# Moving the last attention unit's output into the FFN, the first block's transposes into attention's tail, and one norm's root to GpSimd

## The chip, the cores and the metric

The kernel runs on one core of a Trainium2 chip. A core has five engines that take their own instructions in order: TensorE (PE, matmuls into the eight PSUM banks), VectorE (DVE), ScalarE (ACT, activations by table), GpSimd (POOL) and SyncE (SP, whose queue issues most of the DMAs). They wait for each other by semaphores. The metric is the device time of one execution in microseconds (us). Three runs of the kernel before took 3608.94, 3609.37 and 3612.33 us; the median is 3609.37.

## The reference

One layer of a transformer over 4096 tokens of width 256, in f32: attention with 16 heads, a post-norm, a gated FFN with ternary weights and two hidden layers of 1024, and a second post-norm.

```python
proj = quant4(x) @ ternary_weight(Wqkv_w).T + Wqkv_b
q = proj.reshape(B, N, h, dk).transpose(0, 2, 1, 3)
k = proj.reshape(B, h, N, dk)
v = proj.reshape(B, h, N, dk)
q, k = (rotary(q, N), rotary(k, N))
ql, kl = (q @ U, k @ U)
att = jnp.einsum('bhnr,bhmr->bhnm', ql, kl) / math.sqrt(dk)
y = jax.nn.softmax(att, axis=-1) @ v
y = y.transpose(0, 2, 1, 3).reshape(B, N, d)
x = _layernorm(x + quant4(y) @ ternary_weight(Wo_w).T)
...
h = jax.nn.silu(_tlin(x, w1_w, w1_s)) * _tlin(x, w2_w, w2_s)
h = jax.nn.gelu(_tlin(h, h1_w, h1_s), approximate=False)
h = jax.nn.gelu(_tlin(h, h2_w, h2_s), approximate=False)
x = _layernorm(x + _tlin(h, w3_w, w3_s))
```

`quant4` rounds each row to integers from -8 to 7 by its largest magnitude. `_layernorm` subtracts the mean and divides by the square root of the variance plus 1e-5. `_tlin` is a product with a weight matrix, scaled per output.

## The kernel before

**Attention** works on 64 units: a unit is a pair of heads (8 pairs) and a block of 512 queries (8 blocks). A unit has 32 steps, one for each 128 keys. At a step, `largest` finds the largest score of some rows (PE, then DVE's reduction at L605), and 40 steps later (`LAG`) `weights` computes the scores anew with that largest subtracted (PE, L643) and ACT takes the exponential into a tile `pr` (L651) of the pool `ppool`, which has eight buffers. `values` multiplies two steps' exponentials by the values (PE, L665) at the odd steps, 5 steps behind, into the bank `av`.

When a unit's values are complete, its output is put in order: `finish` (ACT copies `av` into `ya`, L680), eight calls of `turn` (DVE transposes `ya` into `yt` in 32x32 squares, L686), `gather` (SP writes `yt` to DRAM as `y_raw` in four DMAs, L694, and reads it back as `y4`, L699), `add_strips` (POOL adds two halves, L707) and `divide` (DVE takes the reciprocal of the softmax's sum, L716; POOL multiplies, L718; SP stores to `y_dram`, L724).

The order of all this is written out by hand. `at(step, f)` puts a function into a list of that step; the loop at L890 runs over the steps, calls the listed functions and then issues `largest` and `weights`. On each engine the instructions stand in the order in which this loop issues them. `last` is the step number 2048, where the last unit's `largest` ends; the loop goes on to step `last` + 47, with the `weights` of the last 40 steps up to `last` + 39. This stretch is the tail. For the units before the last the pieces of the output's ordering are spread over later steps; for the last unit (`gap` = 0) they come at once, at steps `last` + 45 and `last` + 47.

The tail also prepares the first block of the FFN, 512 tokens. `front_steps(0)` gives seven pieces, put at steps `last` + 2 to `last` + 22: the attention result is quantised on DVE, transposed on PE, multiplied by the output weights, added to x, and normalised: `measure` (mean and variance on DVE, L212), `root` (ACT's square root, L216) and `scale` (DVE, L220 and L222).

**The FFN** follows in a branch: a flag that attention's checks of the weights have set chooses the form (L1055). With these inputs it is the form `split`, in which each f32 operand is held as two f32r parts, high and low. It runs over eight blocks of 512 tokens, again in an order written out by hand. A block has gates (eight pairs of products with w1 and w2, by `o` = 0 to 7; Silu on ACT, product on DVE), two hidden layers h1 and h2 (eight products each with Gelu) and the last layer w3 (two products). A product's matmuls are at L945 and take one of eight PSUM banks. `parts` writes the high part (ACT or DVE, L927) and the low part (DVE, L929). `transpose_x` turns a block of x for the gates (eight PE transposes, L961); for block 0 it stands first in the FFN (L1004). The `front_steps` of the next block are spread over the present block: its load of `y_dram` (`yb`, SP) behind gate `o` = 4, its quantisation behind h1's `o` = 1, its transposes behind `o` = 4.

The weights are loaded by `load_weights` on POOL's queue: w1, w2 and h1 during attention; h2 (4 MB) and w3 (1 MB) at L911 to L913 when the FFN begins, into memory that attention frees. The first half of h2 waits for the last reading of the keys, the second for that of the values.

Of the kernel before, what the change touches and what calls it, by code (L numbers as in the profile page):

```python
# [18 lines left out]
P = 128  # L19
N = 4096  # L20
D = 256
# [16 lines left out]
def attn_ffn_kernel(  # L38
# [31 lines left out]
    make_identity(nc, ident)  # L70
    identb = const.tile([P, P], BF16, name="identb")
    make_identity(nc, identb)

    identr = const.tile([P, P], F32R, name="identr")
    nc.gpsimd.tensor_copy(identr, ident)
    ones = const.tile([P, P], F32, name="ones")
    nc.gpsimd.memset(ones, 1.0)
    eps = const.tile([P, 1], F32, name="eps")
    nc.gpsimd.memset(eps, LN_EPS)

    most = const.tile([P, BT, 2], F32, name="most")
    nc.gpsimd.memset(most, 1e-6)
# [118 lines left out]
    def load_x(b):  # L201
        nc.sync.dma_start(out=xs[b], in_=x_t[:, ts(b, BT), :])

    def layernorm_steps(t):

        mv = stat.tile([P, BT, 2], F32, name="mv")
        sd = stat.tile([P, BT], F32, name="sd")

        def measure():
            for i in range(BT):  # L210
                st = stat.tile([P, 6], F32, name="st")
                nc.vector.bn_stats(st, t[:, i, :])  # L212
                nc.vector.bn_aggr(mv[:, i, :], st)

        def root():
            nc.scalar.activation(sd, mv[:, :, 1], AF.Sqrt, bias=eps)  # L216

        def scale():
            rs = stat.tile([P, BT], F32, name="rs")
            nc.vector.reciprocal(rs, sd)  # L220
            for i in range(BT):
                nc.vector.tensor_scalar(  # L222
                    t[:, i, :],
                    t[:, i, :],
                    mv[:, i, 0:1],
                    rs[:, i : i + 1],
                    ALU.subtract,
                    ALU.mult,
                )

        return measure, root, scale

    def front_steps(b, bank):

        xb = xs[b]
        yb = quantp.tile([P, BT, D], F32, name="yb")
        nc.sync.dma_start(out=yb, in_=y_dram[b].rearrange("(t p) d -> p t d", p=P))

        def evacuate(i, ps, ma7):
            o = quantp.tile([P, D], F32, name="o", bufs=2)  # L240
            nc.vector.scalar_tensor_tensor(o, ps, ma7, alpha_o, ALU.mult, ALU.mult)
            nc.gpsimd.tensor_tensor(xb[:, i, :], xb[:, i, :], o, ALU.add)

        held, biggest, measure_y, quantized, transposed = quantize_steps(yb, bank, nc.vector)

        def integers():
            biggest(None)
            for f in measure_y:
                f()
            quantized()  # L250

        measure, root, scale = layernorm_steps(xb)
        return [
            integers,
            transposed,
            lambda: project(held, sgn_o, bank, 0, evacuate),
            lambda: project(held, sgn_o, bank, 2, evacuate),
            measure,
            root,
            scale,  # L260
        ]


    with ExitStack() as actx:
# [23 lines left out]
        m_dram = [dram.tile([32, P], F32, name=f"m_dram{i}") for i in range(2)]  # L288

        qpool = actx.enter_context(tc.tile_pool(name="qpool", bufs=2))  # L290
        ppool = actx.enter_context(tc.tile_pool(name="ppool", bufs=8))
        ps_sc = actx.enter_context(tc.tile_pool(name="ps_sc", bufs=2, space=PSUM))
        ps_av = actx.enter_context(tc.tile_pool(name="ps_av", bufs=1, space=PSUM))
        ps_1 = actx.enter_context(tc.tile_pool(name="ps_1", bufs=3, space=PSUM))
# [290 lines left out]
        def at(step, f):  # L585
            todo.setdefault(step, []).append(f)
# [89 lines left out]
        def finish(u):  # L676


            yas[u] = qpool.tile([P, QB], F32, name="ya", bufs=1)
            nc.scalar.copy(yas[u], avs.pop(u))  # L680
            yts[u] = qpool.tile([P, QB], F32, name="yt", bufs=1)

        def turn(u, i):

# [3 lines left out]
        def gather(u):  # L688

            del yas[u]  # L690
            raw = y_raw[u % 2]
            yt = yts.pop(u).rearrange("p (b e) -> p b e", e=32)
            for strip in range(4):
                nc.sync.dma_start(  # L694
                    out=raw.rearrange("(b q) s e -> s q b e", q=32)[strip],
                    in_=yt[32 * strip : 32 * strip + 32],
                )
            y4s[u] = qpool.tile([P, BT, 2, 2, 32], F32, name="y4", bufs=1)
            nc.sync.dma_start(  # L699
                out=y4s[u].rearrange("p t j k e -> p t (j k e)"),  # L700
                in_=raw.rearrange("(t p) s e -> p t (s e)", p=P),
            )

        def add_strips(u):
            y4 = y4s.pop(u)
            ys[u] = qpool.tile([P, BT, 2, DK + 1], F32, name="y", bufs=1)
            nc.gpsimd.tensor_tensor(  # L707
                ys[u], y4[:, :, :, 0, : DK + 1], y4[:, :, :, 1, : DK + 1], ALU.add
            )

        def divide(u):

            pair, qb = divmod(u, NQB)
            y = ys.pop(u)
            den = stat.tile([P, BT, 2], F32, name="den")
            nc.vector.reciprocal(den, y[:, :, :, DK])  # L716
            yu = stat.tile([P, BT, 2, DK], F32, name="yu")
            nc.gpsimd.tensor_tensor(  # L718
                yu,
                y[:, :, :, :DK],  # L720
                den.unsqueeze(3).broadcast_to([P, BT, 2, DK]),
                ALU.mult,
            )
            nc.sync.dma_start(  # L724
                out=y_dram[qb].rearrange("(t p) d -> p t d", p=P)[
                    :, :, pair * 32 : (pair + 1) * 32
                ],
                in_=yu.rearrange("p t j e -> p t (j e)"),
            )
# [33 lines left out]
        with tc.manual_schedule():  # L763
# [70 lines left out]
            for u in range(NU):  # L834
# [18 lines left out]
                at(NKT * (u + 1) + 3, lambda u=u: largest_rows(u))  # L853
                end = base + NKT + AVLAG - 1
                at(end, lambda u=u: finish(u))
                gap = 2 if u < NU - 1 else 0
                for i in range(8):
                    at(end + 2 + gap * i, lambda u=u, i=i: turn(u, i))
                at(end + 2 + 8 * gap, lambda u=u: gather(u))
                at(end + 4 + 11 * gap, lambda u=u: add_strips(u))  # L860
                at(end + 4 + 12 * gap, lambda u=u: divide(u))
            last = NKT * NU
            at(last - 240, lambda: load_weights(w1_sb, w1T, 0))
            w2_sb, h1_sb, h2_sb = [None, None], [None, None], [None, None]
# [19 lines left out]
            def start_front():  # L884
                steps = front_steps(0, lambda shape, dt: ps_1.tile(shape, dt, name="ps1"))
                for i, f in zip((0, 6, 10, 12, 16, 18, 20), steps):
                    at(last + 2 + i, f)

            at(last - 60, start_front)
            for s in range(NKT * NU + LAG + AVLAG + 4):  # L890
                while todo.get(s):
# [10 lines left out]
    with ExitStack() as fctx:  # L902
# [4 lines left out]

        h2_sb[0] = kpool.tile([P, NC // 2, DH], F32R, name="h2a", tag="kT")
        h2_sb[1] = wpool2.tile([P, NC // 2, DH], F32R, name="h2b")
        w3_sb = wpool2.tile([P, NC, D], F32R, name="w3_sb")  # L910
        for i in range(2):  # L911
            load_weights(h2_sb[i], h2T, i * NC // 2)
        load_weights(w3_sb, w3T, 0)  # L913

        def bank(shape, dt):
            return psum.tile(shape, dt, name="ps_mm")
# [1 line left out]
        def ffn(split):  # L918
# [2 lines left out]
            np_ = 2 if split else 1  # L921
            dt = F32R if split else F32
            nb = NT // BT

            def parts(dst, k, g, eng):

                eng(dst[:, k, 0, :], g)  # L927
                if split:
                    nc.vector.tensor_tensor(  # L929
                        dst[:, k, 1, :], g, dst[:, k, 0, :].bitcast(F32), ALU.subtract  # L930
                    )

            def product(w, o, src):
                ps = bank([P, 512], F32)
# [16 lines left out]
                        )  # L951
                return ps

            xTs, fTs = {}, {}

            def transpose_x(b):
                xTs[b] = tmp.tile([P, 2, np_, BT * P], dt, name="xT", bufs=1)
                for k in range(2):
                    ps = bank([P, 512], F32)
                    for i in range(BT):  # L960
                        nc.tensor.transpose(ps[:, ts(i, P)], xs[b][:, i, ts(k, P)], ident)  # L961
                    parts(xTs[b], k, ps, nc.scalar.copy)

            def gates(b, o, ha):
                pa = product(((w1_sb,), w1T), o, xTs[b])
# [9 lines left out]
            def hidden(w, sc, o, ha, hb):  # L975
                ps = product(w, o, ha)
                g = tmp.tile([P, BT * P], F32, name="gate", bufs=3) if split else hb[:, o, 0, :]
                nc.scalar.activation(g, ps, AF.Gelu, scale=scales[sc][:, o : o + 1])  # L978
                if split:
                    parts(hb, o, g, nc.vector.tensor_copy)  # L980

            def last_layer(b, o, ha):
                ps = product(((w3_sb,), w3T), o, ha)
# [17 lines left out]
            def hlayer():  # L1001
                return hpool.tile([P, NC, np_, BT * P], dt, name="h")

            transpose_x(0)  # L1004
            for b in range(nb):
                fronts = ends = None
                ha = hlayer()
# [1 line left out]
                for o in range(NC + 1):  # L1009

                    held, g = g, gates(b, o, ha) if o < NC else None
                    if o and split:
                        parts(ha, o - 1, held, nc.scalar.copy)
                    if b and o < 2:
                        add_up(b - 1, o)
                    if o == 4 and b + 1 < nb:
                        fronts = front_steps(b + 1, bank)
                if b:
                    ends = layernorm_steps(xs[b - 1])
                hb = hlayer()  # L1020
                for o in range(NC):
                    hidden((h1_sb, h1T), "hs1", o, ha, hb)
                    if o == 0 and ends:
                        ends[0]()
                    if fronts:
                        step = {1: 0, 4: 1, 5: 2, 6: 3, 7: 4}.get(o)
                        if step is not None:
                            fronts[step]()
                ha, hb = hb, hlayer()
                for o in range(NC):  # L1030
# [12 lines left out]
                    if o == 1 and b + 2 < nb:  # L1043
                        load_x(b + 2)
                    if o == 3 and b + 1 < nb:
                        transpose_x(b + 1)
                for o in range(2):
                    last_layer(b, o, hb)
            for o in range(2):
# [67 lines left out]
```

## Time and profile before

| what | value |
|---|---|
| median of three runs | 3609.37 us |
| the profiled execution: time, span | 3610.68 us, 3608.9 us |
| mean granted TensorE clock | 0.989 |
| busy: PE, DVE, ACT, POOL | 3553.8, 3044.0, 2340.4, 429.1 us |
| last exponential of the tail starts | 2911.95 us |
| last matmul of attention ends | 2914.1 us |
| first matmul of h1, block 0 | 2948.50 us |
| DMA rate, 2920 to 2930 us | 291 GB/s |

Times within the profile are counted from the start of the span. In a row of instructions the first two numbers are the start and the duration; then come the engine, the line of the kernel, the operation, what it writes and reads with the shapes, and how many were merged. What stands in brackets is how long the engine was idle before, and what ended that. In the chain of work that ended last, each piece is followed back to what released it. PEclk is the share of TensorE's full clock that was granted in that stretch.

### The profile page before, as it was taken

How to read it: one execution, taken by the hardware profiler on the slowest of the kernel's cores; microseconds unless marked ns; L12 is line 12 of the kernel's file. 1: busy time of each engine (PE TensorE's matmuls, PEld its weight loads, DVE VectorE, ACT ScalarE, POOL GpSimd, SP SyncE). 2: the span in 40 equal slices, each digit the busy share in tenths (PEclk: the TensorE clock that was granted, in tenths of full speed). 3: DMA queues.
4: the chain of work that ended last, by engine and by line, in shares of the span. 5: the costliest groups of instructions: out<-in, count | busy, mean ns of one | idle time of the engine just before them, and what ended most of it. 6: DMA issues, size and time to landing. Idle time of an engine off the chain costs nothing.

```text
span 3608.9 us, 61076 instructions
## 1 busy us (share of the span) xinstructions
PE 3553.8 (98%) x23831; PEld 2000.3 (55%) x23831; DVE 3044.0 (84%) x5611; ACT 2340.4 (65%) x2715; POOL 429.1 (12%) x515
## 2 busy tenths in 40 slices
PE   8999999999999999999999999999999979999998
PEld 4444555555545555555555555455555458888887
DVE  8888999999999999999999999999999735555544
ACT  2777777777777777777777777777777743333333
POOL 5666300000000000000000000000000000000000
PEclk7999999999999999999999999999999989999999
DMA  3343212111211121111111111200221030000000
GB/s 88 93 111 101 59 26 50 26 27 26 53 29 27 27 50 28 28 42 34 26 26 44 34 29 28 50 21 21 55 59 38 15 89 1 24 30 18 18 7 13
DMA packets 267634, 141.74 MB, mean 39 GB/s; under 512 B 184520, under 2 KB 243656, under 8 KB 266440
## 3 DMA queue, kind: packets, MB, share of 16 engines
q1 hardware_dynamic: 263512, 126.22, 14.0%
q0 software_dynamic: 3824, 11.54, 1.0%
q8 instruction: 189, 3.10, 0.4%
q14 instruction: 109, 0.89, 0.1%
HBM read 91.44 MB, written 42.07 MB: 37 GB/s over the span
## 4 chain that ended last, share of the span: by engine, by line
PE 93%; DVE 2%; DMA 2%; POOL 2%; ACT 1%; issue 0%; SPq 0%; POOLq 0%; DVEq 0%; ACTq 0%
PE av L665 27%; PE sc L643 25%; PE ps L597 21%; PE ps_mm L945 18%; DVE mx L605 1%; PE ps L494 0%; DMA qT<-q_dram 0%; DMA y_raw<-yt 0%; DMA ma_dram<-ma_turned 0%; DMA kT<-k_dram 0%; PE ps L424 0%; DMA scale<-ma_dram 0%; POOL qk L457 0%; PE sc L523 0%; PE ps L171 0%
## 5 line engine op out<-in xcount | busy, mean ns | idle before, releaser
L605 DVE TENSOR_REDUCE mx<-ps 128x1 f32<-128x512 f32 x4096 | 2549.8, 682 | 149.0 <-PE ps L597 94.3
L651 ACT ACTIVATE pr<-sc 128x1024 f32<-128x1024 f32 x2048 | 1991.4, 1021 | 739.4 <-PE sc L643 737.5
L597 PEld LDWEIGHTS ps<-kT,qT 64*128 64x128 f32 x4096 | 568.7, 185 | 983.4 <-DVE mx L605 851.2
L665 PE MATMUL av<-pr,v_all 128*32 128x512 f32 x8192 | 1091.9, 605 | 0.0
L597 PE MATMUL ps<-kT,qT 64*128 64x512 f32 x4096 | 1068.2, 475 | 6.2 <-DMA qT<-q_dram 1.7
L643 PE MATMUL sc<-m_rows,minus 64*128 64x512 f32 x4096 | 823.7, 395 | 3.9 <-ACT pr L651 3.5
L643 PE MATMUL sc<-qT,kT 64*128 64x512 f32 x4096 | 818.2, 392 | 0.0
L643 PEld LDWEIGHTS sc<-m_rows,minus 64*128 64x128 f32 x4096 | 393.6, 185 | 91.7 <-ACT pr L651 40.9
L643 PEld LDWEIGHTS sc<-qT,kT 64*128 64x128 f32 x4096 | 394.0, 185 | 86.5
L665 PEld LDWEIGHTS av<-pr,v_all 128*32 128x32 f32 x8192 | 161.4, 108 | 257.9 <-issue 256.1
L978 ACT ACTIVATE gate<-ps_mm,sc_hs 128x512 f32<-128x512 f32 x128 | 88.0, 688 | 288.9 <-PE ps_mm L945 248.5
L927 DVE CAST h<-gate 128x512 fp32r<-128x512 f32 x128 | 54.3, 425 | 223.7 <-ACT gate L978 223.6
L618 POOL TENSOR_TENSOR m_parts<-m,m_parts 128x8 fp32r<-128x8 f32 x64 | 12.9, 202 | 1800.3 <-ACT m_parts L617 1765.1
L929 DVE TENSOR_TENSOR h<-gate,h 128x512 fp32r<-128x512 f32 x192 | 132.3, 689 | 5.1
L686 DVE STREAM_TRANSPOSE yt<-ya 128x64 f32<-128x64 f32 x512 | 118.1, 232 | 17.9 <-ACT ya L680 17.9
L945 PE MATMUL ps_mm<-h,h1a 128*128 128x512 f32 x512 | 128.9, 394 | 0.0
L945 PE MATMUL ps_mm<-h,h2a 128*128 128x512 f32 x512 | 127.2, 390 | 0.0
L945 PE MATMUL ps_mm<-h,h2b 128*128 128x512 f32 x512 | 126.5, 389 | 0.0
L945 PE MATMUL ps_mm<-h,h1b 128*128 128x512 f32 x512 | 126.5, 389 | 0.0
L970 DVE SCALAR_TENSOR_TENSOR gate<-ps_mm,sc_s,gate 128x512 f32<-128x512 f32 x64 | 48.0, 750 | 83.2 <-ACT gate L968 58.0
L945 PEld LDWEIGHTS ps_mm<-h,h1b 128*128 128x128 f32 x512 | 96.1, 188 | 20.1
L945 PEld LDWEIGHTS ps_mm<-h,h2b 128*128 128x128 f32 x512 | 96.1, 188 | 20.0
(160 smaller groups left out, 1640.9 us busy)
## 6 DMA issues: line engine op xcount, KB each, us to landing
y_raw<-yt SPq DMA_DIRECT2D x256, 64.0 KB
y<-y_raw SPq DMA_DIRECT2D x64, 256.0 KB
qT<-q_dram SPq DMA_DIRECT2D x252, 64.0 KB
kT<-k_dram SPq DMA_DIRECT2D x28, 512.0 KB
xs<-in_x SPq DMA_DIRECT2D x16, 512.0 KB
q_dram<-qk SPq DMA_DIRECT2D x32, 256.0 KB
k_dram<-qk SPq DMA_DIRECT2D x56, 128.0 KB
cs_q<-in_csq SPq DMA_DIRECT2D x8, 512.0 KB
```

The costliest lines, as they stand in the source:

```text
L597: nc.tensor.matmul(ps[j], lhsT=qTs[u][rows, ts(qt, P)], rhs=kTs[u // NQB][rows, ts(ck, 512)], start=True, stop=True,)
L605: nc.vector.tensor_reduce(mxs[u][:, qt, j, ck : ck + 1], ps[j], AX.X, ALU.max)
L618: nc.gpsimd.tensor_tensor(parts[:, :, 1, :], m, parts[:, :, 0, :].bitcast(F32), ALU.subtract)
L643: nc.tensor.matmul(ps[:, j, :], lhsT=minus[rows, :] if first else kTs[u // NQB][rows, ts(kt, P)], rhs=m_rows[u % 2][rows, :] if first else ...
L651: nc.scalar.activation(pr, ps, AF.Exp)
L665: nc.tensor.matmul(avs[u][strip : strip + 32, :], lhsT=v_all[:, 2 * (2 * pair + j) + a, c * (DK + 1) : c * (DK + 1) + 32], rhs=probs[s + k ...
L686: nc.vector.transpose(yts[u][:, ts(i, 64)], yas[u][:, ts(i, 64)])
L927: eng(dst[:, k, 0, :], g)
L929: nc.vector.tensor_tensor(dst[:, k, 1, :], g, dst[:, k, 0, :].bitcast(F32), ALU.subtract)
L945: nc.tensor.matmul(ps, lhsT=sb[:, ks, ts(o, P)] if split else wo[:, k, :], rhs=src[:, k, i, :], start=(k == 0 and i == 0), stop=(k == n - ...
L970: nc.vector.scalar_tensor_tensor(g, pb, scales["s2"][:, o : o + 1], gate, ALU.mult, ALU.mult)
L978: nc.scalar.activation(g, ps, AF.Gelu, scale=scales[sc][:, o : o + 1])
```

## The change

1. The last unit's output is no longer ordered in attention's tail, apart from ACT's copy `ya`. Its turns, its DMAs, its addition and its division go into the first block of the FFN: the turns and `gather` behind gate `o` = 1, `add_strips` behind h1's `o` = 2, `divide` behind `o` = 3. Its tiles come to lie in memory that lives on: `ya` and `y4` in the third buffer of x, `yt` in a tile of the quantisation.
2. Block 0's x is transposed in the tail, at steps `last` + 28 and `last` + 30, into the memory of w3, which moves into a pool that lives from the start; DVE writes the high part there instead of ACT. w3 is loaded behind block 0's gates. To make room, `ppool` has six buffers instead of eight and `yu` two instead of four.
3. The root of block 0's first norm is taken by POOL: variance plus 1e-5, raised to the power -0.5, then two rounds of four operations that refine it. ACT's square root and DVE's reciprocal go for this one norm.
4. An identity in f32r that nothing used goes; a constant of -0.5 comes.

```diff
-    identr = const.tile([P, P], F32R, name="identr")
-    nc.gpsimd.tensor_copy(identr, ident)
...
+    minus_half = const.tile([P, BT], F32, name="minus_half")
+    nc.gpsimd.memset(minus_half, -0.5)
...
-    def layernorm_steps(t):
+    def layernorm_steps(t, between=False):
...
         def root():
-            nc.scalar.activation(sd, mv[:, :, 1], AF.Sqrt, bias=eps)
+            if not between:
+                nc.scalar.activation(sd, mv[:, :, 1], AF.Sqrt, bias=eps)
+                return
+            nc.gpsimd.tensor_scalar(sd, mv[:, :, 1], LN_EPS, None, ALU.add)
+            r = stat.tile([P, BT], F32, name="rs")
+            nc.gpsimd.tensor_tensor(r, sd, minus_half, ALU.pow)
+            for _ in range(2):
+                e = stat.tile([P, BT], F32, name="rse")
+                nc.gpsimd.tensor_tensor(e, r, r, ALU.mult)
+                nc.gpsimd.tensor_tensor(e, e, sd, ALU.mult)
+                nc.gpsimd.tensor_scalar(e, e, -0.5, 1.5, ALU.mult, ALU.add)
+                nc.gpsimd.tensor_tensor(r, r, e, ALU.mult)
+            inv.append(r)
...
-        measure, root, scale = layernorm_steps(xb)
+        measure, root, scale = layernorm_steps(xb, b == 0)
...
+    def transpose_x(b, k, xT, split, bank, eng):
+        ps = bank([P, 512], F32)
+        for i in range(BT):
+            nc.tensor.transpose(ps[:, ts(i, P)], xs[b][:, i, ts(k, P)], ident)
+        parts(xT, k, ps, split, eng)
+
+    left = []
+
+    w3_sb = wpool.tile([P, NC, D], F32R, name="w3_sb")
+    xTs = {0: w3_sb.rearrange("p (k i a) d -> p k i (a d)", k=2, i=2)}
+    last_unit = x_bufs[2].rearrange("p i d -> p (i d)")
...
-        ppool = actx.enter_context(tc.tile_pool(name="ppool", bufs=8))
+        ppool = actx.enter_context(tc.tile_pool(name="ppool", bufs=6))
...
+        def turn_last():
+            yas[NU - 1] = last_unit[:, :QB]
+            yts[NU - 1] = quantp.tile([P, BT * D], F32, name="yt", tag="qtmp")[:, :QB]
+            for i in range(8):
+                turn(NU - 1, i)
+            gather(NU - 1)
...
-                gap = 2 if u < NU - 1 else 0
+                if u == NU - 1:
+                    left += [turn_last, lambda u=u: add_strips(u), lambda u=u: divide(u)]
+                    continue
...
+                def first_xT(k):
+                    transpose_x(0, k, xTs[0], True, bank1, nc.vector.tensor_copy)
+
+                for k in range(2):
+                    at(last + 28 + 2 * k, lambda k=k: first_xT(k))
...
-        w3_sb = wpool2.tile([P, NC, D], F32R, name="w3_sb")
         for i in range(2):
             load_weights(h2_sb[i], h2T, i * NC // 2)
-        load_weights(w3_sb, w3T, 0)
...
-            transpose_x(0)
+            if not split:
+                next_xT(0)
...
                     if o and split:
-                        parts(ha, o - 1, held, nc.scalar.copy)
+                        parts(ha, o - 1, held, split, nc.scalar.copy)
+                    if not b and o == 1:
+                        left[0]()
...
+                if not b and split:
+                    load_weights(w3_sb, w3T, 0)
...
+                    if not b and o in (2, 3):
+                        left[o - 1]()
```

More of the change, by code (lines that the diff above doesn't have):

```diff
@@ L202, in load_x @@
         nc.sync.dma_start(out=xs[b], in_=x_t[:, ts(b, BT), :])
-    def layernorm_steps(t):
+    def layernorm_steps(t, between=False):
         mv = stat.tile([P, BT, 2], F32, name="mv")
         sd = stat.tile([P, BT], F32, name="sd")
+        inv = []
         def measure():
@@ L215, in root @@
         def root():
-            nc.scalar.activation(sd, mv[:, :, 1], AF.Sqrt, bias=eps)
-        def scale():
-            rs = stat.tile([P, BT], F32, name="rs")
-            nc.vector.reciprocal(rs, sd)
+            if not between:
[11 more added lines that the diff above has]
+            inv.append(r)
+        def scale():
+            if between:
+                rs = inv.pop()
+            else:
+                rs = stat.tile([P, BT], F32, name="rs")
+                nc.vector.reciprocal(rs, sd)
             for i in range(BT):
@@ L261, in front_steps, with parts @@
         ]
+    def parts(dst, k, g, split, eng):
+        eng(dst[:, k, 0, :], g)
+        if split:
+            nc.vector.tensor_tensor(dst[:, k, 1, :], g, dst[:, k, 0, :].bitcast(F32), ALU.subtract)
+    def transpose_x(b, k, xT, split, bank, eng):
[7 more added lines that the diff above has]
+    last_unit = x_bufs[2].rearrange("p i d -> p (i d)")
     with ExitStack() as actx:
@@ L676, in finish @@
         def finish(u):
-            yas[u] = qpool.tile([P, QB], F32, name="ya", bufs=1)
+            if u < NU - 1:
+                yas[u] = qpool.tile([P, QB], F32, name="ya", bufs=1)
+            else:
+                yas[u] = last_unit[:, :QB]
             nc.scalar.copy(yas[u], avs.pop(u))
-            yts[u] = qpool.tile([P, QB], F32, name="yt", bufs=1)
+            if u < NU - 1:
+                yts[u] = qpool.tile([P, QB], F32, name="yt", bufs=1)
+        def turn_last():
[4 more added lines that the diff above has]
+            gather(NU - 1)
         def turn(u, i):
@@ L697, in gather @@
                 )
-            y4s[u] = qpool.tile([P, BT, 2, 2, 32], F32, name="y4", bufs=1)
+            if u < NU - 1:
+                y4s[u] = qpool.tile([P, BT, 2, 2, 32], F32, name="y4", bufs=1)
+            else:
+                y4s[u] = last_unit[:, QB:].rearrange(
+                    "p (t j k e) -> p t j k e", t=BT, j=2, k=2
+                )
             nc.sync.dma_start(
@@ L705, in add_strips @@
             y4 = y4s.pop(u)
-            ys[u] = qpool.tile([P, BT, 2, DK + 1], F32, name="y", bufs=1)
+            if u < NU - 1:
+                ys[u] = qpool.tile([P, BT, 2, DK + 1], F32, name="y", bufs=1)
+            else:
+                ys[u] = y4[:, :, :, 0, : DK + 1]
             nc.gpsimd.tensor_tensor(
@@ L716, in divide @@
             nc.vector.reciprocal(den, y[:, :, :, DK])
-            yu = stat.tile([P, BT, 2, DK], F32, name="yu")
+            yu = stat.tile([P, BT, 2, DK], F32, name="yu", bufs=2)
             nc.gpsimd.tensor_tensor(
@@ L855, in attn_ffn_kernel @@
                 at(end, lambda u=u: finish(u))
-                gap = 2 if u < NU - 1 else 0
+                if u == NU - 1:
+                    left += [turn_last, lambda u=u: add_strips(u), lambda u=u: divide(u)]
+                    continue
                 for i in range(8):
[L858 to L861, printed above, removed]
+                    at(end + 2 + 2 * i, lambda u=u, i=i: turn(u, i))
+                at(end + 18, lambda u=u: gather(u))
+                at(end + 26, lambda u=u: add_strips(u))
+                at(end + 28, lambda u=u: divide(u))
             last = NKT * NU
@@ L923, in ffn @@
             nb = NT // BT
[L925 to L931, printed above, removed]
             def product(w, o, src):
@@ L952, in product, with next_xT @@
                 return ps
-            xTs, fTs = {}, {}
-            def transpose_x(b):
+            fTs = {}
+            def next_xT(b):
                 xTs[b] = tmp.tile([P, 2, np_, BT * P], dt, name="xT", bufs=1)
                 for k in range(2):
[L959 to L962, printed above, removed]
+                    transpose_x(b, k, xTs[b], split, bank, nc.scalar.copy)
             def gates(b, o, ha):
@@ L979, in hidden @@
                 if split:
-                    parts(hb, o, g, nc.vector.tensor_copy)
+                    parts(hb, o, g, split, nc.vector.tensor_copy)
             def last_layer(b, o, ha):
@@ L1045, in ffn @@
                     if o == 3 and b + 1 < nb:
-                        transpose_x(b + 1)
+                        next_xT(b + 1)
                 for o in range(2):
```

## The prediction

> **What bounds the kernel now.** I first read the page's strip of forty slices (90.2 us each). TensorE (PE) is at 9 tenths in nearly all of them. What the change can win lies where it is not: in the eighth slice from the right, 2887 to 2977 us, where attention gives over to the FFN and the granted clock dips too. There I read the chain that ended last, in order of time, then the instructions of ScalarE (ACT) in order, then PE's.
>
> The strip, one character a slice:
>
> ```profile
> PE   8999999999999999999999999999999979999998
> PEclk7999999999999999999999999999999989999999
> ```
>
> The chain across the join (start, duration, what):
>
> ```profile
> 2911.85 2.27 PE av L665 x16
> ...
> 2914.15 0.59 ACT ya L680
> ...
> 2914.76 1.14 DVE yt L686 x8
> ...
> 2917.46 10.10 DMA y_raw<-yt
> ...
> 2927.68 2.91 DMA y<-y_raw
> ...
> 2930.73 0.48 POOL y L707
> ...
> 2931.24 0.21 DVE den L716
> ...
> 2931.98 0.70 DVE xT L929
> 2932.68 0.04 issue
> 2932.72 34.07 PE ps_mm L945 x143
> ```
>
> PE's attention work ends at 2914.1 and the FFN's products run from 2932.7. Between them stands the last unit's output: turned, sent to DRAM, fetched, added, divided. No FFN product needs that output; block 7 alone does. It holds PE because VectorE (DVE) takes its instructions in order, and the division's reciprocal (den, L716) stands ahead of the low half of the first block's transposed x (xT, L929). PE's own rows, the last of them being the first matmul of the second layer (h1):
>
> ```profile
> 2916.19 0.50 PE L945 MATMUL ps_mm<-xT,w_sb 128*128 128x512 f32 x1 [0.29 <-ACT xT L927]
> 2932.72 1.65 PE L945 MATMUL ps_mm<-xT,w_sb 128*128 128x512 f32 x3 [16.03 <-DVE xT L929]
> ...
> 2948.50 1.98 PE L945 MATMUL ps_mm<-h,h1a 128*128 128x512 f32 x8
> ```
>
> The stop costs twice: the granted clock in the windows of 1 us is 0.50 from 2932 to 2935, and three matmuls take 1.65 us where four take 1.07 later.
>
> ACT's rows in attention's tail, where the norm's root is:
>
> ```profile
> 2885.20 1.02 ACT L651 ACTIVATE pr<-sc 128x1024 f32<-128x1024 f32 x1 [0.43 <-PE sc L643]
> 2886.24 1.28 ACT L216 ACT_TABLE_LOAD   x1
> 2887.54 0.30 ACT L216 ACTIVATE sd<-mv,eps 128x4 f32<-128x4 f32 x1
> 2887.85 1.28 ACT L651 ACT_TABLE_LOAD   x1
> 2889.15 2.94 ACT L651 ACTIVATE pr<-sc 128x1024 f32<-128x1024 f32 x3
> 2893.78 1.94 ACT L651 ACTIVATE pr<-sc 128x1024 f32<-128x1024 f32 x2 [1.69 <-PE sc L643]
> ```
>
> A root of 512 values stops the exponentials for two table loads; PE runs dry behind it, and the granted clock is 0.50 from 2892 to 2894.
>
> **The change part by part.**
>
> *The join, gain 19.2.* Before, from the end of the last av (2914.1) to the first matmul of the second layer (2948.5): 34.4 us. After it, nothing of the last unit stands ahead of the gates, and both halves of xT lie ready. PE's gap from its last av to its next instruction is 0.74 us today, and I keep it. A pair of gate products then costs 1.81 us (w1's products start at 2939.43 and 2941.24); eight pairs are 14.5. New: 0.74 + 14.5 = 15.2; gain 34.4 - 15.2 = 19.2. The FFN's eight transposes in front of the gates are in the 34.4 and so go as well. ACT's Silu table load (1.28 us), which hid in the stop, now stands behind the copy of ya, 0.59 us of copy, some 0.4 of branch (as DVE's two entries L1055 and L1056 took) and the load: 2.3 after av, 1.6 after PE starts. With eight PSUM banks PE needs no bank back before four pairs, 7.2 us: no cost. If that cover were gone it would cost 1.3.
>
> *Where the moved work goes.* Eight turns (1.13 us of DVE) come after the first parts of the gates (o = 1). DVE is asked for 0.75 + 0.68 = 1.43 us per pair of 1.81 there, so it recovers 0.38 a pair, three pairs, within the four of the banks: 0, at worst 1.1. SP (SyncE's queue): the four writes of y_raw start near 2918 (the end of av moves to 2914.1 - 4.3 + 0.9 = 2910.7 by the terms below; then 0.74, two pairs, and 0.75 + 0.69 + 1.13 of DVE); today they took 11.6 us (2915.92 to 2927.56) beside the loads of h2 and w3, and 3.6 for the unit before (2889.89 to 2893.45). So the fetch of y4, and behind it on SP the load of yb of block 1, go out between 2922 and 2930. Who waits: DVE's quantisation of yb, today from 2957.74 to 2962.8 (5.1 us), and PE's transposes of it at 2966.63. Both move 22.6 earlier, the transposes to 2944.0, so yb must be there by 2939, 9 us after the latest issue; a DVE that waits until then is late only for the second layer's outputs, which the third layer needs. POOL's large loads landed in 3.1 to 10.5 us, so 0, at worst 1.5 of PE time. The additions and the reciprocal (hidden layer, o = 2 and 3) come some 10 us after the latest y4 issue, which took 2.9: 0.
>
> *w3.* Its four issues (0.74 us each) move on POOL from the join to behind the gates, where they wait for PE's last reading of xT; behind them on POOL stand the strip addition and the adds of block 1, needed only from 2942 on. Its first use is after both hidden layers, some 58 us later (16 products of 3.63); landing 10.5 at most: 0.
>
> *The root, gain 4.3.* Undisturbed, pairs of exponentials start 2.12 and 2.37 us apart in turn (2898.48, 2900.85, 2902.97, 2905.34). From the exponential at 2885.20 to the last, at 2911.95, there are 21, ten such distances: 22.45, so the last would start at 2907.65. Gain 4.30, of which some 3.0 is ACT's stop and the rest PE's slow clock and refill.
>
> The Trainium skill (ScalarE: Activation LUTs, What ACT_TABLE_LOAD costs) gives a switch of tables 1.28 us of load and 1.38 of drain, 2.66 in all. By it two switches would be an estimated 5.3 for this term and the sum 1.0 larger; the rows show the same load, but the next instruction 0.02 us behind it, so I do not take its figure.
>
> POOL's replacement is ten instructions: an add, the power, and two rounds of four. The nearest rows are POOL's 128x8 operations at 0.20 us (m_parts, L618), so 2.0 us; the other end is POOL's slowest small one, 1.22 us (L345), so 12.2. The mean is ready at 2881.7; the scaling (1.38) must end before PE comes to the first moved transpose. That stands ahead of the scores of an exponential nine after the one at 2885.20, which by those distances starts at 2895.1, its scores some 2 us before: 2893. So POOL has about 10 us. By the near row 8 are left; by the far one PE waits 2.2. I take 0. No row shows a power.
>
> The Trainium skill (GPSIMD Engine Reference, Instruction dispatch) says that the first call to a freshly loaded kernel pays about 6 us. If power were one, the estimate would be 8 us on POOL, still inside the slack, and the sum unchanged; no row of this trace can show it.
>
> *The moved transposes, loss 0.9.* Eight f32 transposes now stand among the tail's scores. Eight take 0.87 to 1.06 us on PE. The nearest row is the output projection in the same tail, twice 0.54: around it pairs go from 2875.14 to 2880.71, 5.6 where two distances are 4.5, so such work is paid in full there. Ends 0 and 1.1; I take 0.9. Their copies (0.43 and 0.69 on DVE, twice) meet a DVE that is idle 6.8 us in this tail: 0.
>
> *Six instead of eight probability buffers.* The exponential of step s overwrites that of s-6, whose av products stand on PE before the scores that this exponential waits for anyway. So 0 by the order in the code; a fault here would be multiplied by 2048. Set-up takes seven of these tiles, and the seventh falls on tw[0], whose readers stand ahead on the same DVE: 0. The identity that goes and the constant that comes are 0.28 and about 0.1 us of POOL, off the chain: 0.
>
> *Sum.* 19.2 + 4.3 - 0.9 = 22.6. The profiled execution took 3610.68 (span 3608.9), 1.3 above the median of 3609.37. 3610.68 - 22.6 = 3588.1, and against the median **3587**.
>
> **The rivals.**
>
> 1. *The gates are slowed by the burst of loads.* Now the gates run while the 4 MB of h2 come in, at a DMA share that was 1.04 in the idle stretch 2920 to 2930. For it: y_raw took 8 us longer there than one unit earlier; code and descriptors of the engines could be late alike, as could yb. Against it: from 2933 to 2938 PE ran gates at a DMA share of 1.0 to 1.1 without gaps. At 8 us late: 22.6 - 8 = 14.6, time 3595.
>
> 2. *POOL's power is late.* With 1.22 us an instruction PE waits 2.2 us; if it is longer still, the root's whole gain goes: 22.6 - 4.3 = 18.3, time 3591.
>
> 3. *The join's wait is replaced.* The first gates might wait for something else: memory of attention's pools under the h and gate tiles, or a bank. For it: PE's first FFN instruction began just as the copy of ya ended (2914.73). Against it: the same row shows this is 0.74 us. If as much as 16 us stayed, the time would be 3603.
>
> 4. *Slower: the probability buffers bind.* If ACT has to wait for a buffer at each step, 2048 exponentials multiply it: 11 ns each (22.6 / 2048) cancels all, 20 ns gives 3587 + 41 = 3628. Against it: the order above, and ACT's waits over the whole span name the scores alone (us in total, times, longest), with no row for av:
>
> ```profile
> ACT pr L651 <- PE sc L643: 737.5, 1020, 2.4
> ```
>
> **How the numbers follow.** My forecast has 0.80, rival 1 0.09, rival 2 0.04, rival 3 0.03, rival 4 0.04. Faster by over 0.2% (7.2 us, about what a measurement of this kernel can tell from no change) are the forecast, rivals 1 and 2, and rival 3 where less stays (0.01): 0.94; within 0.2% the rest of rival 3: 0.02; slower rival 4: 0.04. The range: below, transposes hidden (0.9) and the spread of the runs (0.4 under the median), with a slightly shorter join: 3584. Above, to rival 1 with a little: 3596. That leaves out rival 3, 4 and a tail of the first.
>
> **What would show it.** Right: in the chain, ps_mm L945 follows av within about 1 us and no y_raw stands on it; no table load between the exponentials of the tail; the second layer's first matmul near 2926; the granted clock at 1.00 through the join. Wrong: a PE wait on DVE xs or POOL ahead of the transposes (rival 2), gaps among the gate products (1 or 3), ACT waits on PE av from the first units on, with a pair of steps over today's (4).

## The result, and the profile after

The changed kernel takes 3588.37 us (median; 3586.83 to 3590.5), the kernel before 3609.77 beside it (five runs, the three of the section on its time among them): a ratio of 0.9938, 95% interval 0.9928 to 0.9949, 21.4 us less (18.4 to 26.0 by the interval). The prediction said 3587, with a range of 3584 to 3596.

The profiled execution took 3586.87 us (span 3585.0). In the page's strip of forty slices the dip in the eighth slice from the right is gone from both rows:

```profile
PE   7999999999999999999999999999999999999998
PEclk7999999999999999999999999999999999999999
```

The chain across the join (start, duration, what), which before held the writes and the fetch of the last unit:

```profile
2907.03 2.27 PE av L700 x16
2909.30 0.02 issue
2909.32 0.59 ACT xs L718
2909.92 0.04 issue
2909.96 32.95 PE ps_mm L997 x144
```

PE now goes from attention's last product (av) to the gates with one copy between (ya, which now lies in a buffer of x and bears that name). PE's own rows, start and duration first, as they answer to those shown of before:

```profile
2909.96 1.20 PE L997 MATMUL ps_mm<-w_sb 128*128 128x512 f32 x4 [0.69 <-ACT xs L718]
...
2924.62 1.98 PE L997 MATMUL ps_mm<-h,h1a 128*128 128x512 f32 x8
```

The wait of 16.03 us for DVE is gone; a wait of 0.69 us for the copy ya is left, where it was 0.74. The granted clock is 1.00 in every window that I read from 2890 to 2940 us. The first matmul of h1 comes 15.3 us after the end of av, where it was 34.4. ACT's rows at the place where the table loads stood:

```profile
2883.38 1.94 ACT L686 ACTIVATE pr<-sc 128x1024 f32<-128x1024 f32 x2 [0.43 <-PE sc L678]
2885.50 1.94 ACT L686 ACTIVATE pr<-sc 128x1024 f32<-128x1024 f32 x2 [0.18 <-PE sc L678]
2887.86 1.94 ACT L686 ACTIVATE pr<-sc 128x1024 f32<-128x1024 f32 x2 [0.42 <-PE sc L678]
2889.99 1.94 ACT L686 ACTIVATE pr<-sc 128x1024 f32<-128x1024 f32 x2 [0.19 <-PE sc L678]
2892.35 1.03 ACT L686 ACTIVATE pr<-sc 128x1024 f32<-128x1024 f32 x1 [0.42 <-PE sc L678]
2893.60 1.02 ACT L686 ACTIVATE pr<-sc 128x1024 f32<-128x1024 f32 x1 [0.23 <-PE sc L678]
2895.25 1.03 ACT L686 ACTIVATE pr<-sc 128x1024 f32<-128x1024 f32 x1 [0.63 <-PE sc L678]
2896.51 1.02 ACT L686 ACTIVATE pr<-sc 128x1024 f32<-128x1024 f32 x1 [0.23 <-PE sc L678]
2898.16 1.94 ACT L686 ACTIVATE pr<-sc 128x1024 f32<-128x1024 f32 x2 [0.63 <-PE sc L678]
```

The pairs go on through the root, 2.12 and 2.37 us apart, until the moved transposes split two of them: from 2889.99 to 2898.16 three distances take 8.17, where 2.37 + 2.12 + 2.37 = 6.86 is the rule. That is what the transposes cost in the tail, 1.31 us.

To compare executions without what happens earlier in them, I cut each profile at three marks of the chain: the end of the last load of m_rows (the last unit's score products start then), the end of the last av, and the first matmul of h1. The first stretch is the tail, the second the join; what follows h1's start is 660.3 to 660.4 us in every profile here.

| kernel | tail | join | tail and join | median |
|---|---|---|---|---|
| before | 44.0 | 34.4 | 78.4 | 3609.77 |
| changed | 41.0 | 15.3 | 56.3 | 3588.37 |
| last unit in the tail | 41.3 | 25.9 | 67.2 | 3598.5 |
| only its division in the FFN | 41.0 | 15.3 | 56.3 | 3589.03 |
| transposes in the FFN | 39.7 | 17.3 | 57.0 | 3588.96 |
| root on ACT | 45.5 | 15.4 | 60.9 | 3591.29 |
| last unit's move alone | 42.8 | 17.4 | 60.2 | 3590.76 |
| six buffers alone | 42.7 | 35.5 | 78.2 | 3611.47 |
| long root on POOL | 49.0 | 15.3 | 64.3 | 3596.96 |

Tail and join together give the change 78.4 - 56.3 = 22.1 us. The two profiles differ by 23.9 in span; the other 1.8 lies before the tail, where m_rows has landed at 2868.3 instead of 2870.1. Over all the profiles this mark stands between 2867.3 and 2871.8, and the kernels with the change lie on both sides of the kernel before, so I put it down to the execution and not to the change. The medians, at 21.4, fit that.

The medians come from four series. The kernel before took 3609.77 in the series of the first two rows, 3611.39 in that of the division alone, 3612.46 in that of the last two rows and 3610.1 in that of the others. Against the kernel before of its own series each kernel saves, from the third row down: 11.6, 22.4, 21.1, 18.8, 19.3, 1.0 and 15.5 us. The interval of each such saving is about 4 to 6 us wide to either side (3 for the six buffers), so differences of 2 or 3 us between kernels of the change are read from the profiles, one for each kernel, and the medians neither show nor deny them.

### The profile page after: what moved, and what is told of

Same layout as the page of the kernel before. It is cut to its first block, busy times and chain, and to the rows that moved or that the text cites. A ratio compares the mean times of both kernels' runs of the same rounds, so it can differ in the third digit from the quotient of the medians.

```text
span 3585.0 us, 61100 instructions
## 1 busy us (share of the span) xinstructions
PE 3544.8 (99%) x23824; PEld 1996.1 (56%) x23831; DVE 3044.8 (85%) x5612; ACT 2337.1 (65%) x2710; POOL 432.2 (12%) x525
## 4 chain that ended last, share of the span: by engine, by line
PE 93%; POOL 2%; DVE 2%; DMA 2%; ACT 0%; issue 0%; SPq 0%; POOLq 0%; ACTq 0%
PE av L700 27%; PE sc L678 25%; PE ps L632 21%; PE ps_mm L997 18%; DVE mx L640 1%; DMA qT<-q_dram 1%; DMA scale<-ma_dram 0%; PE ps L529 0%; DMA ma_dram<-ma_turned 0%; POOL eo L469 0%; POOL qk L492 0%; POOL eo L468 0%; DMA q_dram<-qk 0%; POOL rot L484 0%; POOL rot L485 0%
```

## The experiments

**The last unit back in the tail.** Everything else of the change stays.

```diff
-                    left += [turn_last, lambda u=u: add_strips(u), lambda u=u: divide(u)]
+                    at(end + 2, turn_last)
+                    at(end + 4, lambda u=u: add_strips(u))
+                    at(end + 4, lambda u=u: divide(u))
                     continue
...
-                    if not b and o == 1:
-                        left[0]()
...
-                    if not b and o in (2, 3):
-                        left[o - 1]()
```

> The changed kernel with the last unit's turns, transfers, addition and division put back into attention's tail; the transposes in the tail, the root on POOL and the late load of w3 stay. My theory: what held PE at the join is DVE's order, since everything of the gates on DVE then stands behind the last unit's reciprocal (den). That comes about 17 us after the last av, as before. PE can run on into the banks that ACT frees, about nine products (8.8 us after av), and then waits for DVE; seven products remain, at a granted clock of 0.5 at first. So the first matmul of h1 comes 25 to 27 us after av where the changed kernel has 15.3, and the time is 3599 to 3601. Rival, that the transposes' place (and xT's low half) was all that PE waited for: 15.3 us and 3588.4. Second rival, that nothing is won without the move: 34.4 us, less the 2 us of transposes and casts at the head, 3605.

Measured: 3598.5 us (3598.02 to 3599.91), ratio to before 0.9968 (0.9956 to 0.9981); 25.9 us from av to h1. Instructions of all engines at the join, in order of time:

```profile
2918.13 1.07 PE L999 MATMUL ps_mm<-w_sb 128*128 128x512 f32 x4
2922.58 0.38 SPq L750 DMA_DIRECT2D xs<-y_raw  x1
2925.45 0.47 POOL L761 TENSOR_TENSOR xs<-xs 128x136 f32<-128x136 f32 x1 [13.65 <-DMA xs<-y_raw]
2925.96 0.20 DVE L770 RECIPROCAL den<-xs 128x8 f32<-128x8 f32 x1 [14.11 <-POOL xs L761]
...
2926.76 1.41 DVE L1021 SCALAR_TENSOR_TENSOR gate<-ps_mm,sc_s,gate 128x512 f32<-128x512 f32 x2 [0.60 <-DVE den L770]
...
2927.57 2.08 PE L999 MATMUL ps_mm<-w_sb,w 128*128 128x512 f32 x4 [8.37 <-DVE gate L1021]
```

PE makes nine products (2910.74 to 2919.2) and stands for 8.4 us until DVE, which sat 14.1 us at the reciprocal, has emptied a bank. So xT's low half was only the first thing caught behind the reciprocal; with it out of the way the gates' own products on DVE are caught. The median is half a us under the range that I had given, the join within it. With the last unit where it was, the other parts of the change win 8.5 us of the join (34.4 to 25.9), and the last unit's move the other 10.6. Of the 8.5, 7.4 go by the nine products that PE makes before it stops: from its restart to h1 it takes 8.4 us here and 15.8 before. It can make them because the place of the transposes leaves no xT to wait for. The other 1.1 is that PE restarts 17.5 us after av and not 18.6, since the last unit's writes and fetch took less time; w3's load no longer runs beside them, but no run tries that alone.

**Only the division in the FFN.** Turns, writes and fetch of the last unit stand in the tail behind the copy ya; the addition and the division stay behind h1's o = 2 and 3.

```diff
-                    left += [turn_last, lambda u=u: add_strips(u), lambda u=u: divide(u)]
+                    at(end + 2, turn_last)
+                    left += [lambda u=u: y4s.update({u: last_unit[:, QB:].rearrange("p (t j k e) -> p t j k e", t=BT, j=2, k=2)}), lambda u=u: add_strips(u), lambda u=u: divide(u)]
```

> The changed kernel with the last unit's turns and transfers (y_raw, y4) back in the tail, directly behind the copy ya; the addition and the division stay in the FFN behind h1's o = 2 and 3. My theory: of the moved work only the reciprocal waits for the transfers, so moving it alone frees DVE; the turns (1.13 us) come before the gates' first product is there. From av to h1 15.3 us as in the changed kernel, time 3588.4 within the spread of the runs. Rival, that the turns or the transfers ahead of the gates hold something as well (the turns DVE, y_raw in the burst of loads the yb behind it on SP): 17 us or more from av to h1, or a PE wait at block 1's transposes, 3590 to 3596.

Measured: 3589.03 us (3586.53 to 3589.71), ratio 0.9937 (0.9920 to 0.9953); 15.3 us from av to h1, as in the changed kernel. DVE does the turns and then waits for the gates:

```profile
2912.64 1.13 DVE L732 STREAM_TRANSPOSE yt<-xs 128x64 f32<-128x64 f32 x8 [12.64 <-ACT xs L718]
2915.93 1.50 DVE L1020 SCALAR_TENSOR_TENSOR gate<-ps_mm,sc_s,gate 128x512 f32<-128x512 f32 x2 [2.17 <-ACT gate L1018]
```

So of the moved pieces the addition and the division carry the gain, and of these only the reciprocal is on DVE: it is the one instruction ahead of the gates that waits for the transfers. That the addition, which is on POOL, holds no gate is read from the rows and not tried alone: no instruction of the gates is on POOL. Where the turns and the transfers stand does not show in the join or the time.

**The transposes back at the head of the FFN.** The high halves go by ACT, as before; the target is still w3's memory.

```diff
-                for k in range(2):
-                    at(last + 28 + 2 * k, lambda k=k: first_xT(k))
...
-            if not split:
+            if split:
+                for k in range(2):
+                    transpose_x(0, k, xTs[0], True, bank, nc.scalar.copy)
+            else:
                 next_xT(0)
```

> The changed kernel with block 0's transposes back at the head of the FFN (high halves by ACT, as before); the last unit's move, the root on POOL and the late load of w3 stay. My theory: the tail gets back the 1.3 us that pairs of exponentials lost there (three distances took 8.17 where 6.86 is the rule), and the join grows by the transposes, ACT's cast and DVE's two low halves, by the rows of the kernel before about 2.0 us until the first product is complete: net +0.7, time 3589.1, with 17.3 us from av to h1. Rival, that the place of the transposes decided much of the join's 19 us: over 3595. Second rival, that the move cost more than it won: 3587.1.

Measured: 3588.96 us (3588.12 to 3590.93), ratio 0.9941 (0.9925 to 0.9958). The tail is 1.3 us shorter, the join 2.0 longer (17.3), both as expected; the net of 0.7 is within the spread of the runs. PE at the join:

```profile
2912.18 1.06 PE L288 MATMUL ps_mm<-ident,xs 128*128 128x128 f32 x8 [0.74 <-ACT xs L718]
2913.53 0.50 PE L994 MATMUL ps_mm<-w_sb 128*128 128x512 f32 x1 [0.29 <-ACT w_sb L281]
2914.26 1.09 PE L994 MATMUL ps_mm<-w_sb 128*128 128x512 f32 x3 [0.23 <-DVE w_sb L283]
```

Once DVE is free the low half is late by 0.23 us. Beside the last unit's move, the transposes' move into the tail is worth next to nothing.

**The root back on ACT.**

```diff
-        measure, root, scale = layernorm_steps(xb, b == 0)
+        measure, root, scale = layernorm_steps(xb)
```

> The changed kernel with the first norm's root back on ACT (square root, DVE's reciprocal). My theory: +4.3, time 3592.7; of it 2.9 is the stop of the exponentials by two table loads, and the rest PE's half clock and refill behind it, seen as 0.5 in the granted clock for about 2 us. Rival, that only the stop counts: +2.9, 3591.3. Second rival, that the tail is bound by PE and the stop is hidden: 3588.4.

Measured: 3591.29 us (3589.58 to 3593.07), ratio 0.9949 (0.9933 to 0.9966). The profile shows the 4.5 us that my theory wanted (tail 45.5 against 41.0). The medians differ by 2.9 and the savings in their own series by 2.6, nearer to the rival's number; but four runs that spread over 3.5 us decide between 2.9 and 4.3 no more than the interval does. The profile of the next experiment says more.

**The last unit's move alone.** The transposes stand in the FFN and the root on ACT; both edits above together.

> The changed kernel with both the transposes back at the head of the FFN and the root back on ACT, so that of the change only the last unit's move, the late load of w3 and the six buffers remain. My theory: the two costs add, +0.7 and +4.3: 3593.4, which is 16.4 under the kernel before; the move alone brings nearly all of the join's gain. Rival, that the parts need each other (the transposes behind a late norm, or DVE's low halves behind the turns): 3598 or more.

Measured: 3590.76 us (3589.68 to 3592.78), ratio 0.9949 (0.9932 to 0.9966). The join is 17.4, as with the transposes moved back alone. The tail is 42.8: against 39.7 (transposes in the FFN, root on POOL) the root costs 3.1 here, and not 4.3. The median is 2.6 under what I expected, of which the tail explains 1.2; the rest is within the spread. PE's row at the end of the root's stop, and the window of 1 us behind it (after the window and its length: busy time and instructions of PE, PEld, DVE, ACT and POOL, then the granted clock, the DMA share and GB/s), first of the kernel with the root on ACT:

```profile
2887.69 0.79 PE L678 MATMUL sc<-m_rows,minus 64*128 64x512 f32 x2 [3.00 <-ACT pr L686]
```

```profile
2888.00:2889.00 1.00, 1.00 (x8) 0.35 (x10) 0.00 (x0) 0.55 (x1) 0.00 (x0) 0.50 0.64 96
```

and of the last unit's move alone:

```profile
2887.40 0.51 PE L678 MATMUL sc<-m_rows,minus 64*128 64x512 f32 x2 [3.00 <-ACT pr L686]
```

```profile
2888.00:2889.00 1.00, 1.00 (x10) 0.16 (x8) 0.00 (x0) 1.00 (x2) 0.00 (x0) 1.00 0.82 124
```

PE stood for 3.00 us in both. In the profile of before (2.99) and in the first of these the granted clock fell to 0.50 behind that stop; in this one and in that of six buffers, with the same 3.00, it stayed at 1.00. Against the kernel with the same place of the transposes and the root on POOL (39.7 or 41.0), the tails give the root on ACT 4.3 and 4.5 us in the two profiles with the dip, and 3.1 and 3.0 in the two without it. So it costs about 3 us in all four and some 1.4 more where the clock falls. How often it falls, four profiles can't say.

The Trainium skill (TensorE: Matmul & The Clock Gate, What's actually happening) says that the clock is halved after an idle window of about 3.4 us, and that the window runs freely. That one and the same gap is followed by a dip in two profiles and by none in two others fits a window that runs freely; that a gap of 3.00 us, shorter than the page's window, is followed by a dip at all does not, and no run here explains it.

**A long root on POOL.** 14 rounds of refinement instead of 2.

```diff
-            for _ in range(2):
+            for _ in range(14):
```

> The changed kernel with 14 rounds of refinement instead of 2 in POOL's root: 48 more operations at a spacing of 0.285 us, 13.7 us more on POOL. In the changed kernel the scaled block is ready at 2884.98 and PE's first moved transpose starts at 2892.25, so by my reading 7.3 us are slack; PE should wait 6.4 us at the transposes, and with the clock and the refill behind such a stop (1.3 us at ACT's root) the time is 3595 to 3597. Rival, that the slack is much smaller than the rows show and the two rounds already cost something: 3600 and more. Second rival, that the transposes are not bound to the root at all: 3588.4.

Measured: 3596.96 us (3596.38 to 3597.62), 8.6 above the changed kernel; ratio to before 0.9957 (0.9942 to 0.9972). Taken from the savings in their own series, it loses 5.9. In the profile the tail grew by 8.0. PE's row at the first moved transposes, and the windows behind it:

```profile
2899.70 1.45 PE L288 MATMUL ps<-ident,xs 128*128 128x128 f32 x4 [5.22 <-DVE xs L238]
```

```profile
2899.00:2901.00 2.00, 1.30 (x4) 0.73 (x4) 1.77 (x7) 0.00 (x0) 0.19 (x1) 0.50 0.00 0
2901.00:2903.00 2.00, 2.00 (x9) 0.70 (x12) 1.40 (x3) 0.60 (x1) 0.00 (x0) 0.50 0.45 66
2903.00:2905.00 2.00, 2.00 (x12) 0.50 (x4) 0.00 (x0) 0.42 (x1) 0.00 (x0) 0.50 0.44 65
```

PE waits 5.22 us for the scaling, 1.2 less than I expected, and pays 2.8 more at half clock and in the refill, where I had put 1.3. The two misses nearly cancel, so that the time fell into my range is in part luck. The shorter wait has two reasons in the rows. PE began 0.47 us after DVE began to scale (2899.23, four pieces in 1.38 us) and not behind the whole block, so the changed kernel, which scales from 2883.60 and transposes from 2892.25, has 8.2 us to spare and not 7.3; and the 48 operations took 13.4 us and not 13.7. 13.4 - 8.2 = 5.2. So the root has a limit on POOL: it was free because 8.2 us were to spare, and 13.4 more of POOL's time went past that.

**Six buffers in the kernel before.**

```diff
-        ppool = actx.enter_context(tc.tile_pool(name="ppool", bufs=8))
+        ppool = actx.enter_context(tc.tile_pool(name="ppool", bufs=6))
```

> The kernel before with one edit: six probability buffers instead of eight. My theory: no change, 3609.8 within the spread of the runs (about 2 us), since the exponential that overwrites a buffer waits for scores that stand on PE behind that buffer's last reading. Rival: ACT waits for a buffer at the steps; from 11 ns a step on it would show as 22 us and more, 3632.

Measured: 3611.47 us (3608.99 to 3614.01) against 3612.46 for the kernel before in the same series, ratio 0.9999 (0.9990 to 1.0008). The fourth rival is out. (The two buffers of yu were not tried alone.) This profile also shows that the stop at the join has a varying price: its join is 35.5 where that of before is 34.4, and behind PE's restart the granted clock is about 0.5 for some 4.5 us (0.50 from 2930 to 2934, 0.54 in the us after), where it was 0.50 from 2932.72 to 2935 and 0.69 in the us after. In the sum with the tail (78.2 and 78.4) the two varying parts happen to cancel.

## Why the prediction was right, point by point

*The join* (predicted 34.4 to 15.2): 15.3. Its cause held, and two experiments narrow it: DVE's order, and in it the one reciprocal. That the gates stay fed while DVE does the turns held too. The first Silu came later than I wrote, 2.56 us after PE's start and not 1.6, because ACT's table load began only at 2911.23, behind PE's first product by the profile; eight banks covered that as well.

*The tail's root* (4.3): 4.3 in the two profiles, since 44.0 - 41.0 + 1.31 is 4.3. Its part for the slow clock, some 1.4, was read from one execution and is paid only in some, so as a price for any execution it was too large: two of the four profiles with the root on ACT pay about 3.0. That the comparison of the two profiles gives 4.3 again is no second proof, since the dip of before is the very one that I had read it from.

*POOL's chain* (2.0 us by the near row): 3.63, because the power alone took 1.05 us where I took 0.20 for it, and the operations, each waiting for the one before, start 0.285 us apart. POOL's rows:

```profile
2879.93 0.23 POOL L220 TENSOR_SCALAR sd<-mv 128x4 f32<-128x4 f32 x1 [1.38 <-DVE mv L214]
2880.24 1.05 POOL L222 TENSOR_TENSOR rs<-sd,minus_half 128x4 f32<-128x4 f32 x1
2881.37 0.20 POOL L225 TENSOR_TENSOR rse<-rs 128x4 f32<-128x4 f32 x1
2881.65 0.20 POOL L226 TENSOR_TENSOR rse<-rse,sd 128x4 f32<-128x4 f32 x1
```

It cost no time, as I had written; 8.2 us were left by the start of the scaling, 7.3 by its end, of the slack that I put at 8. The Trainium skill (GPSIMD Engine Reference, Instruction dispatch) names some 6 us for the first call to a freshly loaded kernel; the row shows none for the power, which started 0.08 us behind the add. It is the only power of the execution, so no run here shows whether a second one would take less than 1.05.

*The moved transposes* (0.9, ends 0 and 1.1): 1.31, above my upper end. I took 0.44 us for each four of them, by the row of the FFN; in the tail four take 0.59 in the chain, 1.18 for the eight, and they split two pairs of exponentials as well.

*SP, yb and w3* (0): held. The four writes of y_raw went out from 2916.49 and had landed by 2923.24, 6.7 us and between my ends of 3.6 and 11.6. yb went out at 2923.73, DVE took it up at 2933.86 without a wait, and PE's transposes of it came at 2942.76. Beside the burst of h2 (a DMA share of 0.87 from 2911 to 2925) the gates ran at 1.81 us a pair, so the first rival is out for this burst.

*The sum* was 22.6; tail and join gave 22.1 in the profiles and the medians 21.4. The 0.5 to the profiles is nearly all the transposes' term. The 0.7 from there to the medians lies far within their interval (18.4 to 26.0), so no term can be found too large or too small from it.

No version here beats the changed kernel: the one with the transposes in the FFN (0.9941, 0.9925 to 0.9958) and the one that moves only the addition and the division (0.9937, 0.9920 to 0.9953) can't be told from it (0.9938). Of its parts, the last unit's division carries nearly all the time. The root carries about 3 to 4.5 us by the profiles; the medians (3590.76 for the move alone, 3588.37 with the rest) point the same way but don't show it.

## What to carry to other kernels

When a late result holds up the next stage, look for the one instruction that waits for it on an engine whose later work is needed sooner; moving that instruction, here with the addition that feeds it, behind the urgent work won as much as moving the whole chain. Where two things stand behind the same wait, taking one of them away (here xT's low half) shows the next one: 8.5 of 19.1 us were won and the rest stayed. A price read from one stop in one profile holds a part for the clock that other executions may not pay; take the stop itself as the sure part.

## What the runs showed of the hardware that was not expected

- The same stop of PE, 2.99 to 3.00 us, was followed by a granted clock of 0.50 in two profiles and by 1.00 in two others; this goes with 4.3 and 4.5 us for one root on ACT in the first two and 3.0 and 3.1 in the others.
- A power on GpSimd over 128x4 f32 took 1.05 us in each of the five profiles with the root on POOL, five times one of the 0.20 us products beside it; each execution has one such power, its first.
- The same attention code reaches its last unit at 2867.3 to 2871.8 us of the span in nine profiles. Part of that is made in the first 100 us: the granted clock from 80 to 100 us was 0.52 and 0.53 in the profiles of before and of the division alone, and 0.66 to 0.71 in the other seven; the first unit's m_turned came at 84.0 in those two and at 81.9 to 83.3 in the others. Since the division alone is a kernel with the change, the change does not make this difference. What makes the rest stays open.
